# Eleven quads of edges get their rows by one SyncE transfer per edge instead of four GpSimd gathers

## The chip, the cores and the metric

The kernel runs on one core of a Trainium2 chip. A core has five instruction streams that work side by side and wait for one another by semaphores: TensorE (PE, matmul), VectorE (DVE), ScalarE (ACT), GpSimd (POOL) and SyncE (SP), and 16 DMA engines that move data for all of them. The metric is the device time of one execution in microseconds (us).

## What is computed

A graph layer with 12500 nodes and 400000 edges, sorted by destination. All is in 32-bit floats.

```python
h_s, h_v = s @ lin1_ws * a * ..., einsum('nci,cd->ndi', v, lin1_wv) * a * ...   # per node: 160 numbers
hid = silu(edge_scalars @ fc_w1 * _inv(R))                                      # per edge
w1, w2, w3, w4, w5 = split(hid @ fc_w2 * _inv(FC_HID), [64, 128, 160, 192])
es, ev = h_s[edge_src], h_v[edge_src]                                           # gather by source
m_s1 = w1 * es * e0
m_s2 = w4 * einsum('eci,ei->ec', ev, e1) * _inv(3)
m_v1 = (w2 * es)[:, :, None] * e1[:, None, :]
m_v2 = w3[:, :, None] * ev * e0[:, :, None]
m_v3 = w5[:, :, None] * cross(ev, e1[:, None, :]) * _inv(2)
agg = segment_sum(concatenate([...]), edge_dst) * inv_nn                        # scatter by destination
pre = self_connection + agg @ lin2 * a
out = layernorm(x + concatenate([silu(pre_s[:, :64]), sigmoid(pre_s[:, 64:96])[:, :, None] * pre_v]))
```

The row of a source node, 160 floats or 640 bytes, has to be fetched once per edge. This fetch is what the change is about.

## The kernel before

**Stages.** First the node table `h_tab` (12500 rows of 640 bytes, in HBM) is made, with the transposed node features loaded in blocks, some 80 us. Then comes the edge loop, which fills nearly all of the span. At its end the last nodes are normalised and written.

**The edge loop.** 400000 edges are 3125 tiles of 128. Four tiles are a *quad*, and one pass of the loop (`for n, (c, i, tiles) in enumerate(steps)`) handles a quad; there are 782. Six quads are a *chunk* of 24 tiles, for which the edge scalars come as one tile `es` of 128 partitions (two buffers, two transfers of 384 KB, L228). Indices (`idx`, L184) and edge features (`eat`, L185) come for 72 tiles at a time, also into two buffers.

For quad n the loop does this, in order:

- `fetch(n + 4)` asks for what quad n + 4 needs of `es`, `idx` and `eat`.
- `gather` (L423) has GpSimd issue four indirect DMAs (L427), each of which fetches 128 rows of `h_tab` by the indices of one tile into the buffer `hg`. `hg` has four buffers, so GpSimd can be up to four quads ahead of the products that read them.
- `weights` (L432) has TensorE make the edge weights in PSUM, `pw` (L440). `pw` has two buffers.
- `select_quad` (L498) has VectorE write a one-hot of the destinations into spare columns of `pw` (L504) and multiply it by the edge features into `sel` (L507).
- `products` (L444) has VectorE multiply `pw` by `hg` into `pr`: one wide product (L450) and three more (L458). Between them VectorE adds finished blocks into the accumulator `acc` (L546).
- `sum_up` for the quad two before has TensorE multiply `sel` by `pr` into `pa` (L514), which is the sum by destination inside a block of three tiles.
- `hide(n + 2)` has TensorE and ScalarE make the hidden layer of a later quad (L418, L420) on every second quad.
- Finished blocks are copied from `pa` (L709, ScalarE), transposed (L523, TensorE), copied again (L526, L528), multiplied by the second weights (L538) and copied (L541). Nodes whose sums are complete are normalised in groups of four tiles (`finish`, L549): loads of `x` (L562), stores of the result (L614) after L611. Now and then a piece of the self connection is added (L683, L685, L689, L690).

**What sets the order.** TensorE, VectorE, ScalarE and GpSimd run the loop in the order in which it is written (`manual_schedule`, L781). SyncE is not in that list: the order of its loads and stores there is set by the scheduler. Register loads for the places in `acc` are made on VectorE (L733: up to 16 values for one group of blocks).

Of the kernel before, what the change touches and what calls it, by code (L numbers as in the profile page):

```python
# [10 lines left out]
F32 = mybir.dt.float32  # L11
I32 = mybir.dt.int32
I16 = mybir.dt.int16
BF16 = mybir.dt.bfloat16
AF = mybir.ActivationFunctionType
OP = mybir.AluOpType
AX = mybir.AxisListType
ENG = mybir.EngineType
PSUM = bass.MemoryType.PSUM

P = 128
# [3 lines left out]
D = S + V3  # L25
# [6 lines left out]
Q = 4  # L32
# [2 lines left out]
CT = 2 * SIDE  # L35
AHEAD = 3 * CT
NF = 4

MARGIN = 128
NO = 16  # L40
# [13 lines left out]
def gnn_kernel(  # L54
# [21 lines left out]
    nc = tc.nc  # L76
    N = x.shape[0]
# [3 lines left out]
    GT = src.shape[2]  # L81
# [7 lines left out]
    h_tab = dram.tile([N, D], F32, name="h_tab")  # L89
# [7 lines left out]
        engines={ENG.PE, ENG.DVE, ENG.Activation, ENG.Pool, ENG.SP}))  # L97
# [65 lines left out]
    steps = []  # L163
# [10 lines left out]
    def ahead(t):  # L174
        a0 = t // AHEAD * AHEAD
        if a0 not in aheads:
            n = min(AHEAD, TT - a0)
            idx = loads.tile([P, AHEAD], I32, name="idx")
            eat = loads.tile([P, AHEAD, 4], F32, name="eat")
            k = 0  # L180
            while k < n:
                g, u = divmod(a0 + k, GT)
                m = min(n - k, GT - u)
                nc.sync.dma_start(idx[:, k:k + m], src[g][:, u:u + m])  # L184
                nc.sync.dma_start(eat[:, k:k + m].rearrange("p t k -> p (t k)"),  # L185
                                  ea[g].rearrange("p t k -> p (t k)")[:, 4 * u:4 * (u + m)])
                k += m
            aheads[a0] = a0, idx, eat
        return aheads[a0]

    def index(t):
        a0, idx, _ = ahead(t)
        return idx[:, t - a0:t - a0 + 1]
# [26 lines left out]
    def load_chunk(c):  # L220
        if c in ess:
            return
        t0, halves = chunks[c]
        es = ess[c] = loads.tile([2 * S, SIDE * P], F32, name="es")
        for half, n in enumerate(halves):
            to = es[half * S:(half + 1) * S]
            e0 = (t0 + half * halves[0]) * P
            nc.sync.dma_start(to[:, :n * P], es_t[:, e0:e0 + n * P])  # L228
# [34 lines left out]
    with tc.tile_pool(name="nodes", bufs=len(starts)) as nodes, tc.tile_pool(  # L263
        name="nodes_ps", bufs=6, space=PSUM
# [40 lines left out]
        for c0, cn, quarters, cq, xa, xz in loaded:  # L305
# [6 lines left out]
            for t0 in range(0, nt, U):  # L312
                ps = nps.tile([P, U, P], F32, name="hp")
                for t in range(t0, min(t0 + U, nt)):
                    n = min(P, cn - t * P)
                    nc.tensor.matmul(ps[:n, t - t0], xa[:, t * P:t * P + n], l1,
                                     start=True, stop=True)
                k = min(U, full - t0)
# [3 lines left out]
                if t0 + k < nt <= t0 + U:  # L322
                    n = cn - full * P
# [4 lines left out]
            k = quarters * V  # L328
            for u in range(-(-cq // P)):
                n = min(P, cq - u * P)  # L330
# [10 lines left out]
            if cn > full * P:  # L341
                n = cn - full * P
# [29 lines left out]
    for to, part, pieces, w, r0, c0, by in maps:  # L372
        for k, piece in enumerate(pieces):
# [3 lines left out]
            m = terms.setdefault((to, part, four), len(terms))  # L377
# [31 lines left out]
    def hidden(pool, psum, es, halves, t0, n):  # L409
# [5 lines left out]
        for k, c0, c1 in ((2 * S, 0, ends[1]), (S, ends[1], ends[0])):  # L415
            if c1 > c0:
                c = slice(c0 * P, c1 * P)
                nc.tensor.matmul(ph[:k, c], w1[:k, :k], es[:k, t0 * P + c0 * P:t0 * P + c1 * P],  # L418
                                 start=True, stop=True)
                nc.scalar.activation(hid[:k, c], ph[:k, c], AF.Silu, scale=1.0 / math.sqrt(64))  # L420
        return hid

    def gather(pool, idx):  # L423

        hg = pool.tile([P, Q, D], F32, name="hg")
        for t, i in enumerate(idx):
            nc.gpsimd.indirect_dma_start(  # L427
                out=hg[:, t, :], out_offset=None, in_=h_tab,
                in_offset=bass.IndirectOffsetOnAxis(ap=i, axis=0))
        return hg  # L430

    def weights(psum, hid, slots):  # L432

        pw = psum.tile([P, Q, 256], F32, name="pw")
        n = len(slots)
        for t in range(0, n, 2):
            half, c = slots[t]
            m = min(2, n - t)
            assert half == 0 and all(slots[t + k] == (k, c) for k in range(m))
            nc.tensor.matmul(pw[:, t:t + m, :NWT], hid[:m * S, c * P:(c + 1) * P], w2[:m * S, :m],  # L440
                             start=True, stop=True)
        return pw
# [105 lines left out]

    def finish(fin, psum, t0, nt, p, most=NF):  # L549

# [27 lines left out]
        def gates():  # L578
            z, sg = held[:2]
            nc.scalar.activation(sg[:, :nt], z[:, :nt, :V3], AF.Sigmoid)  # L580

# [21 lines left out]
        def root():  # L603
            mv, rs = held[4:]
            nc.scalar.activation(rs[:, :nt], mv[:, :nt, 1], AF.Sqrt, bias=eps)  # L605

        def norm():
# [12 lines left out]
    tiles_of_nodes = -(-N // P)  # L620
    LAST = NF
    jobs = [(t, min(NF, tiles_of_nodes - LAST - t), P)
            for t in range(0, tiles_of_nodes - LAST, NF)]
    last_job = (tiles_of_nodes - LAST, LAST, N - (tiles_of_nodes - 1) * P)

    with tc.tile_pool(
        name="fin", bufs=1
    ) as fin, tc.tile_pool(
        name="late", bufs=2
    ) as late, tc.tile_pool(name="edge", bufs=2) as edge, tc.tile_pool(  # L630
        name="deep", bufs=4
    ) as deep, tc.tile_pool(name="pw_ps", bufs=2, space=PSUM) as pw_ps, tc.tile_pool(
        name="pa_ps", bufs=2, space=PSUM
# [24 lines left out]
        def fetch(n):  # L658

            if n < len(steps):  # L660
                c, i, tiles = steps[n]
                if i == 0:
                    load_chunk(c)
                for t, _, _ in tiles:
                    ahead(t)

        def hide(n):

# [109 lines left out]
                    turning.extend(job[:nt])  # L778
                    doing.extend(job[nt:])

        with tc.manual_schedule(engines={ENG.PE, ENG.DVE, ENG.Activation, ENG.Pool}):  # L781
            fetch(0)
            hide(0)
            waits = []
            pieces = list(range(0, N, CHN))
            products_due = []
            checks = farthest(late)
            for n, (c, i, tiles) in enumerate(steps):
                if 2 <= n < 2 + ZP // 2:
                    for k in range(2):  # L790
                        clear(2 * (n - 2) + k)
                if n in checks:
                    checks[n]()
                fetch(n + 4)
                hg = gather(deep, [index(t) for t, _, _ in tiles])
                pw = weights(pw_ps, hids[c, i // 2], [(half, u - i // 2 * 4) for _, half, u in tiles])

                rest = turning.pop(0)() if turning else None
                step_on = not rest and doing.pop(0) if doing and not turning and not rest else None
                ready = []  # L800

                def first(n=n):
                    if rest:
                        rest()
                    ready.extend(add_up(n))

                sel = select_quad(edge, tiles, pw)
                pr = products(edge, pw, hg, len(tiles), [first, lambda n=n: ready.extend(add_up(n))])
                for a in ready:
                    add(*a)  # L810
                if step_on:
                    step_on()
                begin()
                waits.append((tiles, pr, sel))
                if len(waits) > 2:
                    sum_up(n, *waits.pop(0))
                hide(n + 2)
                for blocks, in due(maps_due, n):
                    output(n, blocks)
                for j, sa in due(turns_due, n):  # L820
                    turn_blocks(n, j, sa)
                if products_due:
                    products_due.pop(0)()()
                if n % 30 == 13 and pieces:
                    products_due.extend([lambda: (lambda: None)] * 3 + self_connection(pieces.pop(0)))
            assert not pieces and not products_due
            last_steps = finish(fin, misc_ps, *last_job, most=LAST)
            n = len(steps)
            while waits:
                sum_up(n, *waits.pop(0))  # L830
            while turns_due or maps_due:
                n += 1
                for blocks, in due(maps_due, n):
                    output(n, blocks)
                for j, sa in due(turns_due, n):
                    turn_blocks(n, j, sa)
            assert len(adds) <= NO
            n += 2
            while adds:
                for a in add_up(n) + add_up(n):  # L840
                    add(*a)
            while turning or doing or to_do:
                begin()
                for f in turning:
                    f()()
                for f in doing:
                    f()
                turning.clear()
                doing.clear()
            for f in last_steps[:LAST]:  # L850
                f()()
            for f in last_steps[LAST:]:
                f()
# [4 lines left out]
        with tc.For_i(0, n_redo, 1):  # L858
# [9 lines left out]
            with tc.For_i(0, n_again, 1) as g, tc.For_i(0, GT, 1) as k:  # L868
                t = g * GT + k
# [20 lines left out]
                hg = gather(deep, [idx])  # L890
# [12 lines left out]
                with tc.For_i(first, last + 1, W) as base:  # L903
# [10 lines left out]
                    nc.vector.tensor_scalar_add(r, r, -float(W))  # L914
            for pool, job, most in [(fin, job, NF) for job in jobs] + [(fin, last_job, LAST)]:
                job_steps = finish(pool, misc_ps, *job, most=most)
# [50 lines left out]
```

## Time and profile before

| | |
|---|---|
| median of three runs | 5207.48 us (5172.77 to 5221.05) |
| the profiled execution | 5221.05 us, of which the span from first to last instruction is 5219.2 us |
| mean granted TensorE clock in it | 0.872 |
| busy: TensorE, VectorE, ScalarE, GpSimd | 77%, 47%, 18%, 57% of the span |
| gathers | 3125, from 78.9 to 5176.5 us after the start |
| moved by DMA | 411.78 MB, 256.20 MB of it by the gathers' queue |

How to read the profile: it is one execution as the hardware profiler recorded it. A line of the groups has the source line, the engine, the operation, what it writes and reads, how often, then busy time in us, the mean of one in ns, and the idle time of that engine just before these instructions with what ended most of it. "issue" is idle time in which the engine waited for nothing that the profile shows; "remote" is a wait that a semaphore ended of which no instruction was found just then. Starts and ends of matmuls are partly modelled. A timeline's lines start with the start and the duration in us. The engine names with a q (SPq, DVEq) are the instructions of that engine's sequencer, such as issuing a DMA or loading registers.

### The profile page before, as it was taken

The page shows a single profiled execution, that of the slowest core. Times are in us where ns is not written, and L with a number is a line of the kernel's source. Part 1 is how long each engine was busy: PE and PEld are TensorE (multiplying, and loading weights), DVE is VectorE, ACT ScalarE, POOL GpSimd, SP SyncE. Part 2 cuts the span into 40 slices and gives each one's busy share as a digit, 9 for nine tenths or more (in the row PEclk, how much of TensorE's full clock was granted, in tenths as well). Part 3 has the DMA queues.
Part 4 walks back from the last instruction along what each step waited for, and adds up shares of the span by engine and source line. Part 5 has one row for each costly group of instructions (what it writes and reads, how often), then busy time and mean ns, then how long its engine had stood idle before and what let it go on. Part 6 is the DMA issues. An engine that isn't in the chain of part 4 may idle for free. (4 is left out here: it accounts for less than half of the span.)

```text
span 5219.2 us, 47675 instructions
## 1 busy us (share of the span) xinstructions
PE 4008.8 (77%) x14291; PEld 1714.8 (33%) x14291; DVE 2436.4 (47%) x6584; ACT 924.8 (18%) x2463; POOL 2980.2 (57%) x3134
## 2 busy tenths in 40 slices
PE   5777777787787877867777787877877787777776
PEld 3333333333333333333333333333333333333333
DVE  4444444444444444545445444444444444444544
ACT  1211111211111111211111111111111111111112
POOL 3565555555555556655556555555555555566563
PEclk7888888898888988889988888888888898889898
DMA  7333333333323323323333333333333333333322
GB/s 189 72 73 76 78 75 79 77 76 80 75 71 77 84 68 80 85 69 85 75 74 86 73 77 82 75 77 79 78 74 78 77 76 79 75 73 86 73 71 50
DMA packets 241214, 411.78 MB, mean 79 GB/s; under 512 B 74201, under 2 KB 171877, under 8 KB 240821
## 3 DMA queue, kind: packets, MB, share of 16 engines
q0 software_dynamic: 150000, 256.20, 20.2%
q1 hardware_dynamic: 77666, 142.75, 11.5%
q10 hardware_dynamic: 13282, 9.69, 0.6%
q8 instruction: 118, 1.93, 0.2%
q14 instruction: 148, 1.20, 0.1%
HBM read 392.40 MB, written 16.00 MB: 78 GB/s over the span
## 5 line engine op out<-in xcount | busy, mean ns | idle before, releaser
L427 POOL DMA_INDIRECT hg<-h_tab,idx x3125 | 2975.5, 952 | 2196.6 <-issue 952.4
L440 PE MATMUL pw<-w,hid 128*128 128x448 f32 x3126 | 1523.7, 614 | 309.3 <-issue 113.2
L514 PE MATMUL pa<-pr,sel 128*64 128x416 f32 x6250 | 1383.7, 555 | 118.8 <-issue 72.3
L504 DVE TENSOR_TENSOR pw<-rel,iota 128x64 f32<-128x64 int16 x782 | 181.1, 232 | 2494.8 <-remote 1243.8
L458 DVE TENSOR_TENSOR pr<-pw,hg 128x384 f32<-128x384 f32 x2346 | 1152.4, 545 | 0.1
L440 PEld LDWEIGHTS pw<-w,hid 128*128 128x128 f32 x3126 | 611.4, 213 | 852.7 <-issue 680.7
L514 PEld LDWEIGHTS pa<-pr,sel 128*64 128x64 f32 x6250 | 406.8, 144 | 1030.7 <-issue 959.0
L523 PE MATMUL pt<-ident,sa 128*128 128x128 f32 x2084 | 363.6, 301 | 390.9 <-ACT hid L420 218.5
L709 ACT COPY sa<-pa 128x416 f32<-128x416 f32 x521 | 265.5, 510 | 1944.0 <-remote 793.1
L450 DVE TENSOR_TENSOR pr<-pw,hg 128x512 f32<-128x512 f32 x782 | 531.0, 679 | 1.5
L418 PE MATMUL ph<-es,w 128*128 128x512 f32 (+1 forms) x784 | 451.5, 658 | 67.4 <-ACT tt L528 35.7
L523 PEld LDWEIGHTS pt<-ident,sa 128*128 128x128 f32 x2084 | 259.5, 152 | 723.3 <-issue 327.5
L538 PE MATMUL po<-tt,l 128*96 128x256 f32 (+5 forms) x1496 | 390.8, 413 | 102.5 <-ACT tt L528 63.7
L420 ACT ACTIVATE hid<-ph 128x512 f32<-128x512 f32 x392 | 234.5, 598 | 1049.7 <-remote 556.5
L507 DVE TENSOR_TENSOR sel<-pw,eas 128x256 f32<-128x256 f32 x782 | 331.5, 424 | 43.8 <-ACT eas L486 0.6
L538 PEld LDWEIGHTS po<-tt,l 128*96 128x96 f32 (+1 forms) x1496 | 249.8, 180 | 267.1 <-issue 96.0
L526 ACT COPY tt<-pt 128x192 f32<-128x192 f32 x521 | 166.0, 319 | 911.2 <-remote 295.9
L418 PEld LDWEIGHTS ph<-es,w 128*128 128x128 f32 x784 | 119.4, 192 | 334.7 <-issue 258.3
L546 DVE TENSOR_TENSOR acc<-acc,os 96x32 f32 x1042 | 194.3, 186 | 25.4 <-ACT os L541 6.9
L528 ACT COPY tt<-pt 128x64 f32<-128x64 f32 x521 | 116.7, 224 | 0.0
L689 PE MATMUL psc<-xv,scv 96*96 96x500 f32 x50 | 39.5, 884 | 82.6 <-ACT hid L420 63.3
L573 PE MATMUL pp<-ident,acc 96*128 96x96 f32 x196 | 37.1, 275 | 82.9 <-DVE acc L546 29.7
(77 smaller groups left out, 674.4 us busy)
## 6 DMA issues: line engine op xcount, KB each, us to landing
es<-in_es_t_dram SPq DMA_DIRECT2D x260, 384.0 KB
hg<-h_tab,idx POOLq DMA_INDIRECT x3125
h_tab<-ht ACTq DMA_DIRECT2D x6, 1280.0 KB
xt<-in_x_dram SPq DMA_DIRECT2D x23, 320.0 KB
out_dram<-y SPq DMA_DIRECT2D x23, 320.0 KB
xv<-in_xv_t_dram SPq DMA_DIRECT2D x25, 187.5 KB
xs<-in_xs_t_dram SPq DMA_DIRECT2D x25, 125.0 KB
xa<-in_xs_t_dram SPq DMA_DIRECT2D x12, 256.0 KB
```

What stands on the lines that cost most here:

```text
L418: nc.tensor.matmul(ph[:k, c], w1[:k, :k], es[:k, t0 * P + c0 * P:t0 * P + c1 * P], start=True, stop=True)
L420: nc.scalar.activation(hid[:k, c], ph[:k, c], AF.Silu, scale=1.0 / math.sqrt(64))
L427: nc.gpsimd.indirect_dma_start(out=hg[:, t, :], out_offset=None, in_=h_tab, in_offset=bass.IndirectOffsetOnAxis(ap=i, axis=0))
L440: nc.tensor.matmul(pw[:, t:t + m, :NWT], hid[:m * S, c * P:(c + 1) * P], w2[:m * S, :m], start=True, stop=True)
L450: nc.vector.tensor_mul(two, pw[:, :n, :2 * S].rearrange("p t (k c) -> p t k c", k=2), hg[:, :n, None, :S].to_broadcast([P, n, 2, S]))
L458: nc.vector.tensor_mul(pr[:, :n, first:first + V3].rearrange("p t (i c) -> p t i c", i=3), pw[:, :n, None, 2 * S + k * V:2 * S + (k + 1) * ...
L507: nc.vector.tensor_mul(sel[:, :n], oh[:, :, None, :].to_broadcast([P, n, 4, W]), by_slot(tiles[0][0])[:, u:u + n, :, None].to_broadcast([P ...
L514: nc.tensor.matmul(pa[half * ROWS:(half + 1) * ROWS, :NPR], sel[:, t].rearrange("p k w -> p (k w)"), pr, start=start, stop=stop)
L523: nc.tensor.transpose(pt[:, four * P:four * P + k], sa[:k, c:c + P], ident[:k, :k])
L538: nc.tensor.matmul(po[:, k, :nb], l2[r, terms[to, part, four]], a[:, :nb], start=(n == 0), stop=(n == len(of) - 1))
L546: nc.vector.tensor_add(window, window, os[:, :, b])
L709: nc.scalar.copy(sa, pas.pop(j)[:, :NPR])
```

## The change

Quads 76, 144, 212 and so on to 756 (every 68th, eleven in all) are no longer gathered by GpSimd. For each of them SyncE

- loads the 4 x 128 indices, one row of 128 per tile, 74 quads before the quad itself (for the first, at the loop's second quad);
- after VectorE has multiplied them by 640 (66 quads before), reads them 16 at a time into registers and issues one transfer of 640 bytes per index from `h_tab` into a buffer of its own, `hq` (one buffer). One such job of 16 rows follows every second quad, 32 jobs for an own quad, so that SyncE is at it in 64 of 68 quads.

`products` then reads `hq` in the place of `hg` for that quad. SyncE is added to the engines that run the loop in the written order.

```diff
+OWN = 68
+BATCH = 16
+EVERY = 2
...
+    own = [n for n in range(OWN + 8, len(steps) - 4, OWN) if len(steps[n][2]) == Q]
+    by_bytes = h_tab.rearrange("n d -> (n d)").bitcast(U8)
+    row_bytes = 4 * D
+
+    def places(pool, n):
+
+        at_bytes = pool.tile([Q, P], I32, name="at_bytes")
+        for k, (t, _, _) in enumerate(steps[n][2]):
+            g, u = divmod(t, GT)
+            with nc.allow_non_contiguous_dma(reason="the indices of one tile"):
+                nc.sync.dma_start(at_bytes[k:k + 1], src[g][:, u:u + 1].rearrange("p u -> u p"))
+        return at_bytes
+
+    def rows_of(pool, at_bytes):
+
+        hq = pool.tile([P, Q, D], F32, name="hq", bufs=1)
+        flat_hq = hq.rearrange("p t d -> p (t d)").bitcast(U8)
+
+        def job(t, p0):
+            _, values = nc.values_load_multi_w_load_instructions(
+                at_bytes[t:t + 1, p0:p0 + BATCH], engines=[ENG.SP], min_val=0,
+                max_val=(N - 1) * row_bytes,
+                skip_runtime_bounds_check_because="every entry of src is the index of a node")
+            for p, v in enumerate(values, p0):
+                nc.sync.dma_start(flat_hq[p:p + 1, t * row_bytes:(t + 1) * row_bytes],
+                                  by_bytes[ds(v, row_bytes)][None])
+
+        return hq, [lambda t=t, p0=p0: job(t, p0) for t in range(Q) for p0 in range(0, P, BATCH)]
...
+        def fetch_rows(n):
+
+            for m in own:
+                if n == max(1, m - OWN - 6):
+                    at_of[m] = places(mine, m)
+                if n == m - OWN + 2:
+                    nc.vector.tensor_scalar_mul(at_of[m], at_of[m], float(row_bytes))
+                    hq_of[m], jobs = rows_of(mine, at_of[m])
+                    rows_due.extend((m, job) for job in jobs)
+            if n % EVERY == 0 and rows_due:
+                rows_due.pop(0)[1]()
+            assert all(m > n for m, _ in rows_due)
...
-        with tc.manual_schedule(engines={ENG.PE, ENG.DVE, ENG.Activation, ENG.Pool}):
+        with tc.manual_schedule(engines={ENG.PE, ENG.DVE, ENG.Activation, ENG.Pool, ENG.SP}):
...
                 fetch(n + 4)
-                hg = gather(deep, [index(t) for t, _, _ in tiles])
+                fetch_rows(n)
+                hg = hq_of.pop(n) if n in own else gather(deep, [index(t) for t, _, _ in tiles])
```

More of the change, by code (lines that the diff above doesn't have):

```diff
@@ L14 @@
 BF16 = mybir.dt.bfloat16
+U8 = mybir.dt.uint8
 AF = mybir.ActivationFunctionType
@@ L628, in gnn_kernel @@
     ) as fin, tc.tile_pool(
+        name="mine", bufs=2
+    ) as mine, tc.tile_pool(
         name="late", bufs=2
@@ L665, in fetch @@
                     ahead(t)
+        at_of, hq_of, rows_due = {}, {}, []
+        def fetch_rows(n):
[9 more added lines that the diff above has]
+            assert all(m > n for m, _ in rows_due)
         def hide(n):
```

## The prediction

> **What bounds the kernel now.** I read the page's busy table first, then its groups, then the waits, then GpSimd's and VectorE's timelines in one stretch. The busy table names no engine that is full:
>
> ```profile
> PE 4008.8 (77%) x14291; PEld 1714.8 (33%) x14291; DVE 2436.4 (47%) x6584; ACT 924.8 (18%) x2463; POOL 2980.2 (57%) x3134
> ```
>
> The groups carry busy time, the mean of one, and the engine's idle time before it:
>
> ```profile
> L427 POOL DMA_INDIRECT hg<-h_tab,idx x3125 | 2975.5, 952 | 2196.6 <-issue 952.4
> L440 PE MATMUL pw<-w,hid 128*128 128x448 f32 x3126 | 1523.7, 614 | 309.3 <-issue 113.2
> L504 DVE TENSOR_TENSOR pw<-rel,iota 128x64 f32<-128x64 int16 x782 | 181.1, 232 | 2494.8 <-remote 1243.8
> L450 DVE TENSOR_TENSOR pr<-pw,hg 128x512 f32<-128x512 f32 x782 | 531.0, 679 | 1.5
> ```
>
> GpSimd does nothing but gathers. 2975.5 + 2196.6 = 5172.1 us lie from the first gather's neighbourhood to the last, so its timeline is the span but for 47 us. Of the idle time 952.4 us is "issue", 0.305 us before each gather, which no one can remove. A gather therefore costs 0.952 + 0.305 = 1.257 us, a quad of four 5.03 us, and the 3125 together 3928 us. The other 1244 us are waits for VectorE to give back an `hg` buffer. VectorE in turn idles 2495 us before L504, its first step of a quad, and only 1.5 us before L450, the first to read gathered rows: it never waits for rows, always for TensorE's `pw`. So each seems to wait for the other. The timelines (start us, duration us, engine and line, idle time before) show how:
>
> ```profile
> 2610.22 1.01 POOL L427 DMA_INDIRECT hg<-h_tab,idx  x1 [5.48 <-DVE acc L546]
> ...
> 2622.79 0.95 POOL L427 DMA_INDIRECT hg<-h_tab,idx  x1 [0.30 <-issue]
> 2624.04 0.95 POOL L427 DMA_INDIRECT hg<-h_tab,idx  x1 [0.30 <-issue]
> 2626.01 0.94 POOL L427 DMA_INDIRECT hg<-h_tab,idx  x1 [1.03 <-DVE acc L546]
> 2627.26 0.95 POOL L427 DMA_INDIRECT hg<-h_tab,idx  x1 [0.30 <-issue]
> 2628.51 0.95 POOL L427 DMA_INDIRECT hg<-h_tab,idx  x1 [0.30 <-issue]
> 2629.77 0.95 POOL L427 DMA_INDIRECT hg<-h_tab,idx  x1 [0.30 <-issue]
> 2635.93 0.94 POOL L427 DMA_INDIRECT hg<-h_tab,idx  x1 [5.21 <-DVE pw L504]
> ```
>
> ```profile
> 2626.82 1.67 PE L440 MATMUL pw<-w,hid 128*128 128x448 f32 x4
> ```
>
> ```profile
> 2615.00 0.23 DVE L504 TENSOR_TENSOR pw<-rel,iota 128x64 f32<-128x64 int16 x1 [0.39 <-PE pw L440]
> 2623.06 0.23 DVE L504 TENSOR_TENSOR pw<-rel,iota 128x64 f32<-128x64 int16 x1 [5.06 <-PE pa L514]
> 2632.97 0.23 DVE L504 TENSOR_TENSOR pw<-rel,iota 128x64 f32<-128x64 int16 x1 [6.91 <-remote]
> ```
>
> GpSimd issues 16 gathers almost without a pause and then stands still. TensorE's `pw` was over at 2628.5, yet L504 starts at 2632.97, 2.25 us after the last gather's end at 2630.72. I counted this over the trace. For each quad whose L504 found VectorE idle, I took the time from the modelled end of its last L440 matmul to L504, and the place of the gather under way in its unbroken run (pauses under 0.5 us). Among the first six gathers of a run, 49 of 271 quads are late by over 0.5 us and the median is 0.04; from the eighth on it is 188 of 190, median 8.7 us. Of all 296 late ones (mean 6.7 us) 120 end between 2.0 and 3.3 us after GpSimd's last gather. I don't know the mechanism, but the order of cause is plain: TensorE's results reach the others late during a long run of gathers, and come when GpSimd runs out of buffers. A turn is then GpSimd's run plus a stall, and a shorter list of gathers shortens the runs.
>
> **The change, part by part.** *Removed:* eleven quads (76, 144, ... 756) lose four gathers each; the built program lists 44 fewer on GpSimd and the same work on TensorE. 44 x 1.257 = 55.3 us of GpSimd's timeline. What becomes of the 1244 us of stalls is not shown. Bounds: they grow by all that is removed, gain 0; or they shrink with the gathers, 44 x (1.257 + 1244/3125) = 72.8. A stall comes when four gathered quads wait, and VectorE must still work through the extra quad (about 2.8 us, which its 47% leaves room for), so I take the stalls as they are: 55.
>
> *Added on VectorE:* eleven multiplications of 4x128 indices. Not in the trace; the nearest rows are 0.17 (L609) to 0.23 us (L504). 2 us, kept on the path since VectorE releases GpSimd. Each also waits for its four index loads, which are issued eight quads (52 us) ahead. Behind it stands that quad's L504, and after it GpSimd. Row loads land in `hq`, and L450 of an own quad waits for them.
>
> *Added on SyncE:* 352 jobs, one in two quads (2 x 5172/782 = 13.2 us), each a load of 16 registers and 16 row transfers; with the 44 index loads that makes 5676 more transfers beside some 640 now. The nearest rows:
>
> ```profile
> L733 DVEq TENSOR_LOAD <-rows x68: 535/1099/2299, 196.9 to 5200.0; - x68
> L185 SPq DMA_DIRECT2D eat<-in_ea_dram x68: 327/423/1495, 65.3 to 4922.1; - x68
> L228 SPq DMA_DIRECT2D es<-in_es_t_dram x262: 465/532/1087, 65.8 to 5128.2; - x131
> ```
>
> L733 reads 1042 / 68 = 15.3 values at a time (durations: shortest/median/longest, ns), so 1.10 us for 16. An issue with the gap to the next (0.05) costs 0.38 to 0.58; a row address in a register is in no row, and I take 0.45. A job is then 1.10 + 16 x 0.45 = 8.3 us, at worst 1.10 + 16 x 0.58 = 10.4. SyncE's own issues add about 0.7 us per job. It fits into 13.2 and hides behind the quads. Without that cover it would be 352 x 8.3 = 2.9 ms.
>
> A limit of another kind: each transfer waits for the one eight before it, as they share eight semaphores. From issue to the last count on its semaphore the trace has 2.05 us for `eat` (median), 4.05 for `idx`, 4.94 for `es` (95%: 6.03). A one-row transfer is nearest to `eat`: 2.05 / 8 = 0.26 per transfer, below the issue. At the end of 6.03 it would be 0.75, a job 13.1.
>
> [...] A gather here moves 80 KB, a row 640 bytes. [...]
>
> *Moved:* SyncE's order is now as written. `es` is asked for four quads before its chunk and read two quads before, 13 us, against 4.94 to land. `idx` is asked for four quads ahead, while GpSimd may gather it one quad later (6.6 us against 4.05). In the old trace an `idx` load went out at 2441 and its edge features were sorted at 2577, 136 us later. SyncE must also pass stores that wait for L611 and the first job of each own quad, which waits for VectorE. A job (8.3) behind such a wait eats most of either margin; GpSimd's lateness there replaces a stall it would have had anyway. I take 0; the price if not is below.
>
> *Sum:* 55 - 2 = 53. The profiled execution took 5221 (span 5219.2), so 5168 for its like. That execution is the slowest of the three and 13.6 above their median, so against the median: 5154.
>
> **Rivals.** *The stalls take it back.* TensorE has the largest share, and if its work sets the pace the eleven quads end no sooner: 5207. For it, 77% and a granted clock of 0.87; against it, L504's lateness follows GpSimd's run. 0.18.
>
> *SyncE falls behind.* The point is a job of 13.2 - 0.7 = 12.5 us, 0.71 per transfer, a landing of 5.7. At 6.03 a job is 13.1 and each of the 352 is 0.6 over: 211 us, everything behind SyncE (`es`, then L418 and all of TensorE) late by it: 5207 + 211 = 5418. For it, `es` lands so late; against it, 384 KB are not 640 bytes. 0.09.
>
> *Late results get later.* If the row transfers lengthen each of the 296 late releases as gathers do, 0.18 us each cancels the gain, and 0.5 us each costs 148: 5154 + 148 = 5302. For it, the cause of lateness is unknown and may be transfers in flight; against it, `es` loads of 768 KB fall in stretches where L504 is prompt (2633.1). 0.08.
>
> *The written order.* 43 `idx` loads and 130 chunks: 1 us late each puts 173 on: 5327. It decides above 0.3 us. For it, margins fall from 136 us to some 26; against it, SyncE runs ahead between waits. 0.07.
>
> That the gathers stay is excluded by the instruction list.
>
> **How the numbers follow.** The forecast gets 0.58. Its own range: stalls shrinking with the gathers, 5207 - 73 + 2 = 5136; half the gain, 5181; three runs spread over 48 us, so 15 more on either side: 5120 to 5195. One per cent of 5207 is 52 us (about what a measurement of this kernel can tell from no change), so the forecast lies on that line, and I put 0.36 of its chance beyond it, as shorter stalls pass it clearly and half the gain is the rarer way to miss. Within 1%: the other 0.22, the first rival's 0.18, and 0.04 for small forms of the other three: 0.44. Slower: the 0.20 left of their 0.24. The range takes the forecast, the first rival and the milder half of the slow cases: 5110 to 5300.
>
> **What would show it.** Right: L427 x3081 with 0.95 and 0.305 as now, its waits for VectorE still near 1240, L450 still without idle time, SyncE's issue near 0.4 us. Wrong: those waits grown by 50 (first rival); the timeline's jobs back to back over 12.5 us (second); mean lateness above 6.7 us (third); L427 waiting for `idx`, or L418 for `es` (fourth).

## The result, and the profile after

The changed kernel took 5392.86 us (median of four runs, 5380.75 to 5413.62), the kernel before 5202.31 beside it: a ratio of 1.0376 [1.0313, 1.0438]. The forecast was 5154, so both its sign and its range (5110 to 5300) missed. The profiled execution after has a span of 5380.5 us against 5219.2. In the changed kernel's numbering L427 is L431, L440 is L473, L450 is L483, L458 is L491, L504 is L537, L546 is L579; the row transfers are L460, their register loads L455.

The busy table and the groups of the kernel after:

```profile
PE 4021.5 (75%) x14291; PEld 1736.1 (32%) x14291; DVE 2438.5 (45%) x6595; ACT 920.3 (17%) x2463; POOL 2938.4 (55%) x3090
```

```profile
L431 POOL DMA_INDIRECT hg<-h_tab,idx x3081 | 2933.6, 952 | 2390.5 <-issue 939.4
L473 PE MATMUL pw<-w,hid 128*128 128x448 f32 x3126 | 1522.8, 615 | 244.8 <-ACT hid L424 138.1
L537 DVE TENSOR_TENSOR pw<-rel,iota 128x64 f32<-128x64 int16 x782 | 180.7, 231 | 2597.5 <-remote 1468.9
L483 DVE TENSOR_TENSOR pr<-pw,hg 128x512 f32<-128x512 f32 x771 | 523.6, 679 | 3.2 <-issue 1.1
```

The 44 gathers are gone and each of the rest costs what it did (952 ns). But GpSimd's waits for others are 2390.5 - 939.4 = 1451 us where they were 1244: +207. With -55 for the gathers that is +152 of the 161 by which the span grew. VectorE waits longer before L537 and still not before L483: it waits for TensorE, not for rows. The waits (us in total, times, longest) show that GpSimd still waits for VectorE's steps above all:

```profile
DVE pw L537 <- remote: 1468.9, 168, 17.5
...
POOL hg L431 <- DVE acc L579: 750.6, 155, 11.5
...
POOL hg L431 <- DVE pr L491: 381.2, 81, 8.7
...
POOL hg L431 <- DMA hq<-h_tab: 61.1, 11, 10.4
...
POOL hg L431 <- DMA idx<-in_src_dram: 8.7, 2, 4.4
```

The last two rows are new: before the change no gather waited for a load of SyncE's. No gather reads `hq`. SyncE's loads share eight semaphores (numbers 100 and 102 to 108 in the trace), and at eight of these 13 waits the gather is the first of a new block of 72 tiles and starts when the index load for it has landed (six of the eight stand under `hq`). Of the +207, then, 70 us stand behind SyncE's loads, 19 behind two waits for a multiplication of indices (L710), and the remaining 118 behind VectorE's usual steps.

One turn in the timelines of GpSimd, VectorE and TensorE after (start, duration, idle time before):

```profile
3196.03 0.94 POOL L431 DMA_INDIRECT hg<-h_tab,idx  x1 [4.82 <-DVE pw L537]
...
3202.28 0.94 POOL L431 DMA_INDIRECT hg<-h_tab,idx  x1 [0.31 <-issue]
...
3209.78 0.95 POOL L431 DMA_INDIRECT hg<-h_tab,idx  x1 [0.30 <-issue]
3216.22 1.01 POOL L431 DMA_INDIRECT hg<-h_tab,idx  x1 [5.49 <-DVE acc L579]
```

```profile
3213.27 0.23 DVE L537 TENSOR_TENSOR pw<-rel,iota 128x64 f32<-128x64 int16 x1 [10.01 <-remote]
```

```profile
3201.70 1.77 PE L473 MATMUL pw<-w,hid 128*128 128x448 f32 x4
```

TensorE's `pw` is over at 3203.5, in the sixth gather of the run (that of 3202.28); L537 starts at 3213.27, 2.5 us after the twelfth and last gather. Before the change a release in the sixth gather was late in 41% of the cases; now it is in 77%. Counted by the gather under way when `pw` ends, as in the prediction:

| gather of the run | 4th | 5th | 6th | 7th | 8th | late ones in all | mean lateness |
|---|---|---|---|---|---|---|---|
| before | .17 | .13 | .41 | .83 | .97 | 296 | 6.70 us |
| after | .23 | .49 | .77 | .92 | .96 | 295 | 6.59 us |

So late releases are neither more nor longer; they begin about one gather earlier. GpSimd also runs dry sooner: runs of 16 gathers fell from 94 to 55, pauses over 0.5 us rose from 292 to 313, and their mean from 4.31 to 4.71 us.

### The profile page after: what moved, and what is told of

Same layout as the page of the kernel before. It is cut to its first block, busy times and chain, and to the rows that moved or that the text cites. A ratio compares the mean times of both kernels' runs of the same rounds, so it can differ in the third digit from the quotient of the medians.

```text
span 5380.5 us, 59309 instructions
## 1 busy us (share of the span) xinstructions
PE 4021.5 (75%) x14291; PEld 1736.1 (32%) x14291; DVE 2438.5 (45%) x6595; ACT 920.3 (17%) x2463; POOL 2938.4 (55%) x3090
## 3 DMA queue, kind: packets, MB, share of 16 engines
q1 hardware_dynamic: 95266, 146.40, 11.7%
## 5 line engine op out<-in xcount | busy, mean ns | idle before, releaser
L431 POOL DMA_INDIRECT hg<-h_tab,idx x3081 | 2933.6, 952 | 2390.5 <-issue 939.4
L473 PE MATMUL pw<-w,hid 128*128 128x448 f32 x3126 | 1522.8, 615 | 244.8 <-ACT hid L424 138.1
L547 PE MATMUL pa<-pr,sel 128*64 128x416 f32 x6250 | 1368.0, 556 | 96.5 <-ACT sa L759 51.1
L537 DVE TENSOR_TENSOR pw<-rel,iota 128x64 f32<-128x64 int16 x782 | 180.7, 231 | 2597.5 <-remote 1468.9
L491 DVE TENSOR_TENSOR pr<-pw,hg 128x384 f32<-128x384 f32 x2313 | 1136.3, 545 | 2.4 <-issue 2.4
L473 PEld LDWEIGHTS pw<-w,hid 128*128 128x128 f32 x3126 | 616.9, 215 | 777.8 <-issue 569.1
L556 PE MATMUL pt<-ident,sa 128*128 128x128 f32 x2084 | 383.1, 313 | 583.3 <-ACT hid L424 277.9
L556 PEld LDWEIGHTS pt<-ident,sa 128*128 128x128 f32 x2084 | 271.5, 158 | 932.4 <-ACT hid L424 319.4
L422 PE MATMUL ph<-es,w 128*128 128x512 f32 (+1 forms) x784 | 464.3, 675 | 133.3 <-ACT tt L561 102.7
L483 DVE TENSOR_TENSOR pr<-pw,hg 128x512 f32<-128x512 f32 x771 | 523.6, 679 | 3.2 <-issue 1.1
L422 PEld LDWEIGHTS ph<-es,w 128*128 128x128 f32 x784 | 121.9, 196 | 400.1 <-issue 251.8
L579 DVE TENSOR_TENSOR acc<-acc,os 96x32 f32 x1042 | 194.0, 186 | 30.5 <-ACT os L574 6.7
L574 ACT COPY os<-po 96x512 f32<-96x512 f32 (+2 forms) x68 | 38.3, 563 | 419.5 <-PE po L571 124.4
```

The costliest lines, as they stand in the source:

```text
L431: nc.gpsimd.indirect_dma_start(out=hg[:, t, :], out_offset=None, in_=h_tab, in_offset=bass.IndirectOffsetOnAxis(ap=i, axis=0))
L483: nc.vector.tensor_mul(two, pw[:, :n, :2 * S].rearrange("p t (k c) -> p t k c", k=2), hg[:, :n, None, :S].to_broadcast([P, n, 2, S]))
L491: nc.vector.tensor_mul(pr[:, :n, first:first + V3].rearrange("p t (i c) -> p t i c", i=3), pw[:, :n, None, 2 * S + k * V:2 * S + (k + 1) * ...
L547: nc.tensor.matmul(pa[half * ROWS:(half + 1) * ROWS, :NPR], sel[:, t].rearrange("p k w -> p (k w)"), pr, start=start, stop=stop)
L556: nc.tensor.transpose(pt[:, four * P:four * P + k], sa[:k, c:c + P], ident[:k, :k])
L579: nc.vector.tensor_add(window, window, os[:, :, b])
```

## The experiments

Each ratio is to the kernel before in the same set of runs. The sets fell into two kinds, and no ratio below can be read without this: in some the kernel before took 5136 to 5219 us, in others 4044 to 4051 (the results name one chip number under both kinds, so it may not be the chip itself). I call them *late* and *prompt*, for the releases of TensorE; the prediction and the result above are of the late kind.

**Parts of the change, late kind.** e1_order is the kernel before with SyncE added to the written order, nothing else.

```diff
-with tc.manual_schedule(engines={ENG.PE, ENG.DVE, ENG.Activation, ENG.Pool}):
+with tc.manual_schedule(engines={ENG.PE, ENG.DVE, ENG.Activation, ENG.Pool, ENG.SP}):
```

> The kernel before, with SyncE's loop in the written order and nothing else changed. Theory A (the row transfers make TensorE's results reach the others late sooner, so that GpSimd's stalls grow by 207 us): no row transfers here, so within 20 us of before (about 5202). Theory B (the written order makes es and idx late): most of the 190 us lost, 5340 to 5400. Theory C (TensorE sets the pace and the gathers removed are worth nothing): as before, 5202.

Measured 1.0021 [0.9997, 1.0046]. By itself the written order costs nothing that stands out of the noise, 24 us at the most.

e2_fewer_gathers has the 44 gathers fewer, but no row transfers: the eleven quads read a buffer that was filled once.

```diff
-                fetch_rows(n)
-                hg = hq_of.pop(n) if n in own else gather(...)
+                hg = hq if n in own else gather(...)
```

> The changed kernel without its row transfers, index loads and multiplications: the eleven quads read a buffer that one plain load of 512 rows fills before the loop, so their products use the wrong rows; GpSimd has 3081 gathers and SyncE the written order. Theory A: the gain of the forecast without its cost, 5202 - 55 = 5147 (5130 to 5170), stalls before L431 near 1240 us. Theory B: 5290 to 5350. Theory C: 5202, the stalls grown by 55.

Measured 0.9957 [0.9924, 0.9991], some 22 us of 5219 (5 to 40), between theory A (a gain of 32 to 72 us) and C (none). The page:

```profile
L431 POOL DMA_INDIRECT hg<-h_tab,idx x3081 | 2937.2, 953 | 2210.6 <-issue 942.8
```

GpSimd's waits are 1268 us: the stalls take back part of the 55, though not all of it.

e3_rows_too keeps all gathers and lets SyncE fetch all the rows as well, for nobody.

```diff
-                hg = hq_of.pop(n) if n in own else gather(...)
+                hg = gather(...)
```

> The changed kernel with all of its row transfers, but GpSimd gathers the eleven quads as well and the products read those; hq is filled and never read. Theory A: the loss of the change without its gain, 5393 + 55 = 5448 (5420 to 5480), late releases from the fifth or sixth gather of a run instead of the seventh or eighth. Theory B: 5393 at most. Theory C: 5393, since the gathers are worth nothing.

Measured 1.0391 [1.0354, 1.0428]. The rows alone cost it all; against the change's 1.0376, of another set, the 44 gathers saved are worth some 8 us, which is within the noise, and not the 55 of theory A:

```profile
L431 POOL DMA_INDIRECT hg<-h_tab,idx x3125 | 2974.8, 952 | 2400.4 <-issue 940.7
```

e4_lighter_pe is the kernel before with half the columns in two of three L514 additions of a block, to see if TensorE's work is the pace.

```diff
+        n = NPR if start else NPR // 2
-        nc.tensor.matmul(pa[..., :NPR], ..., pr, start=start, stop=stop)
+        nc.tensor.matmul(pa[..., :n], ..., pr[:, :n], start=start, stop=stop)
```

> The kernel before with less TensorE work: the second and third tile of each block add only the first 208 of 416 columns into pa, so 208 columns of most sums lack two thirds of their edges. That takes 4166 x 0.174 us = 725 us of matmul at full clock. If TensorE's work sets the pace (C): 4500 to 4600. If GpSimd's runs and the late results set it (A): within 100 us of 5202, since the runs and the place where results turn late are as before.

Measured 1.0017 [0.9982, 1.0053], with TensorE busy for 3745 us instead of 4009: it is not.

**What of the rows costs, late kind.** All three keep every gather, the 44 index loads and the eleven multiplications, and use no row. e6_loads_only has the 352 register loads without transfers; e7_fixed_rows has 5632 one-row transfers with fixed addresses and no register loads; e8_sixteen_rows moves the same bytes in 352 transfers of 16 rows.

```diff
-            _, values = nc.values_load_multi_w_load_instructions(...)   # e7, e8
-            for p, v in enumerate(values, p0):                      # e6: loop left out
+            for p in range(p0, p0 + BATCH):                         # e7
+                v = (t * P + p) * 23 * row_bytes
                 nc.sync.dma_start(flat_hq[p:p + 1, ...], by_bytes[ds(v, row_bytes)][None])
+            r0 = (t * P + p0) * 23                                  # e8
+            nc.sync.dma_start(hq[p0:p0 + BATCH, t], h_tab[r0:r0 + BATCH, :])    # e8
```

> All gathers stay on GpSimd; SyncE loads the indices and does the 352 register loads of 16 values, but issues no row transfer. If the register loads bring the late results on sooner: 5400 to 5430, as with rows and all gathers (1.039). If it is the transfers: 5210 to 5240 (1.000 to 1.005), stalls before L431 near 1270 us.

> All gathers stay on GpSimd; SyncE issues the 5632 transfers of one row in the same bursts of 16, but from addresses fixed when the kernel is built (wrong rows, never read) and without register loads. If the transfers themselves are the cost, whatever their addresses: 5400 to 5440 (1.035 to 1.042). If addresses in registers are: 5210 to 5250.

> All gathers stay on GpSimd; each burst of 16 one-row transfers is one transfer of 16 rows from a fixed address (never read): the same bytes and the same rows of 640 bytes, 352 issues instead of 5632. If the bytes or the rows in flight are the cost: 5400 to 5440. If the count of issues and completions is: 5210 to 5250 (1.000 to 1.006).

Measured 1.0043 [1.0015, 1.0070], 1.0250 [1.0212, 1.0288] and 1.0051 [1.0018, 1.0084]. GpSimd's lines of e7 and then e8:

```profile
L431 POOL DMA_INDIRECT hg<-h_tab,idx x3125 | 2981.1, 954 | 2242.3 <-issue 948.5
```

```profile
L431 POOL DMA_INDIRECT hg<-h_tab,idx x3125 | 2973.8, 952 | 2113.6 <-issue 952.9
```

e7 lies between its two expectations; e6 and e8 came as expected if transfers are the cause. Bytes matter little; the number of transfers does. Not even the packets differ: the queue that brings the rows (q1) moved 95266 of them and 146.40 MB in e7 and in e8 alike, so the cost goes with the issues and completions. (The rows of one transfer in e8 lie side by side in `h_tab`, those of e7 do not.) What takes the step from 1.025 to 1.039 was asked of e14_loads_fixed in a later set of the late kind: register loads and transfers, with fixed addresses.

```diff
             _, values = nc.values_load_multi_w_load_instructions(...)   # kept, unused
-            for p, v in enumerate(values, p0):
+            for p in range(p0, p0 + BATCH):
+                v = (t * P + p) * 23 * row_bytes
```

> The kernel before with all gathers, the index loads, the 352 register loads and 5632 single-row transfers from fixed addresses (loaded values and rows are left unused). Where TensorE's releases come late: 1.034 to 1.040 if the register loads beside the transfers make up the difference between 1.025 (fixed addresses, no register loads) and 1.039 (true addresses with them); 1.025 to 1.030 if true addresses do. Where the releases do not come late: 0.999 to 1.001.

Measured 1.0257 [1.0202, 1.0311]: true addresses make the step, not the register loads. In the trace of the changed kernel a true address puts one more instruction on SyncE for each row, a MOVE into a register ahead of the transfer:

```profile
L460 SPq MOVE hq<-h_tab x5632: 2/29/1422, 153.3 to 5161.4; - x195
```

By the instructions that each has beyond the 47675 of the kernel before (the head of the page), the runs order themselves: e8 +387, 1.0051; e6 +405, 1.0043; e7 +5682, 1.0250; e14 +6047, 1.0257; e3 +11690, 1.0391. The first two are alike within the noise. That the addresses are also scattered was not tried apart from that.

Two things in the traces limit this account. With true addresses SyncE has less time to spare, and index loads come late: GpSimd waited for SyncE's loads for 55 us in e3, 27 in e14 and 16 in e7, so up to half of the step of some 70 us may be this. And the earlier onset of late releases goes with the cost only in part: in the sixth gather 79% are late in e3 and 68% in e14, but 40% in e7, which costs as much as e14; kernels with few transfers of rows or none have 14 to 41%. That the earlier onset is what costs the time is therefore not shown.

**Less buffering.** e5_buffers2 is the kernel before with two `hg` buffers instead of four.

```diff
-         name="deep", bufs=4
+         name="deep", bufs=2
```

> The kernel before with two hg buffers instead of four. If a turn is GpSimd's run of gathers plus a stall of some 6 us, and the late results end with the run: runs of at most 8 to 12 gathers, stalls of 4 to 6 us each, more of them; 6.2 to 8 us for a quad, so 5200 to 6200, and lateness (mean 6.7 us) falls by half. If TensorE set the pace: 5200, unchanged.

Measured, late kind, 0.9915 [0.9884, 0.9946]:

```profile
L427 POOL DMA_INDIRECT hg<-h_tab,idx x3125 | 2980.1, 954 | 2094.2 <-issue 921.9
L504 DVE TENSOR_TENSOR pw<-rel,iota 128x64 f32<-128x64 int16 x782 | 180.0, 230 | 1765.0 <-remote 825.0
```

Less buffering is worth 44 us of 5136, but not in the way expected. The runs did not get shorter (10.8 gathers in the mean, 10.7 before; 81 of them are 16 long) and the mean lateness is 6.8 us instead of half of 6.7. Late releases are fewer, 229 where the profile before has 296 and e8, of this set, 271. What brings the gain is not shown.

**The prompt kind.** The next set was meant to go on from there, with the changed kernel on two buffers (e9), half the fixed rows (e10: eight of each job's sixteen), and three buffers (e12). A fourth run, e11_loads_fixed, is the kernel of e14.

```diff
-         name="deep", bufs=4
+         name="deep", bufs=2        # e9, in the changed kernel; e12: bufs=3, in the kernel before
-            for p in range(p0, p0 + BATCH):         # e10, against e7
+            for p in range(p0, p0 + BATCH // 2):    # e10
```

> The changed kernel with two buffers for the gathered rows instead of four. Theory: the row transfers cost time by bringing the late releases on earlier within long unbroken runs of gathers, so shorter runs leave them less to spoil: in the kernel before, two buffers gave 0.9915 with 229 late one-hots instead of 296. With both, a ratio of 1.010 to 1.025 against the kernel before, and the waits of GpSimd for other engines below 1350 us (1451 in the changed kernel). Rival: the transfers hold TensorE's releases up by themselves, however long the run: then the two effects add, 1.038 less 0.0085, which is 1.027 to 1.033, and the waits stay above 1380.

> The kernel before with all gathers, and SyncE fetching rows at fixed addresses as in the run of 5632 single-row transfers (1.025), but eight in a job instead of sixteen: 2816 transfers in as many jobs. The rows are not used. If each transfer adds its own small hold-up, the cost halves: 1.012 to 1.016. If a few transfers in a run of gathers are enough to bring the late releases on, most of it stays: 1.019 to 1.025. If only a job longer than the gap between two gathers does harm (sixteen transfers took some 5 to 9 us, eight 2.6 to 4), it goes: below 1.008.

> The kernel before with all gathers, the index loads, the 352 register loads and 5632 single-row transfers; the loaded values are left unused and the transfers read fixed addresses (the rows are not used either). Fixed addresses without register loads gave 1.025, true addresses with them 1.039, register loads alone 1.0043. If the rest comes from the register loads beside the transfers, this gives 1.034 to 1.040; if from addresses that are taken from registers or scattered at random over the table, 1.025 to 1.030.

> The kernel before with three buffers for the gathered rows instead of four (two gave 0.9915). If the gain comes from GpSimd's being held sooner, so that its unbroken runs of gathers get shorter, three buffers give part of it: 0.993 to 0.999, with 240 to 285 late one-hots. If two buffers happen to be right for another reason (less held by a pause at each quad), three are no better than four, 0.998 to 1.002, with some 290 late ones.

The kernel before took 4046.34 us here, so that the premise of the four expectations, late releases, did not hold: e9 1.0613 [1.0595, 1.0631], e10 0.9992 [0.9982, 1.0001], e11 0.9992 [0.9982, 1.0001], e12 1.0010 [1.0000, 1.0019]. The page of e12, which is the kernel before but for a buffer, shows what is different:

```profile
L427 POOL DMA_INDIRECT hg<-h_tab,idx x3125 | 2979.1, 953 | 1029.3 <-issue 945.1
L450 DVE TENSOR_TENSOR pr<-pw,hg 128x512 f32<-128x512 f32 x782 | 537.5, 687 | 928.2 <-DMA hg<-h_tab,idx 927.2
L504 DVE TENSOR_TENSOR pw<-rel,iota 128x64 f32<-128x64 int16 x782 | 178.5, 228 | 500.3 <-PE pw L440 497.3
```

A gather costs what it did (953 + 302 ns), but GpSimd waits for others only 84 us, and 3125 x 1.255 = 3922 us of gathers fill a span of 4047. "remote" is gone from L504, three of 282 releases are late, and VectorE now waits for gathered rows (L450). GpSimd runs for up to 1116 gathers without a pause. So a long run of gathers does not make TensorE late by itself, and where nothing is late the rows are free (e11: 0.9992).

That the change itself is then a gain was tested by running it again. The first time fell into the late kind:

> The changed kernel once more, beside a run on whose chip the kernel before took 4046 us instead of some 5200, with GpSimd issuing its gathers almost without a pause (3125 x 1.257 us is 3928) and no late releases of TensorE. Theory: the change costs time only by way of the late releases. Where they occur, 1.033 to 1.044, as measured at first. Where they do not, the 44 gathers saved show in full and the rows cost nothing: 55 of 4046 us less, a ratio of 0.984 to 0.990. Rival: the rows or their use (the product that waits for a quad's last row, the multiply, the index loads) cost time of their own: then 1.00 or more there as well.

1.0345 [1.0291, 1.0400], as at first. The second time fell into the prompt one, with half the rows beside it:

> The changed kernel again, beside the run with half the rows. Where TensorE's releases come late: 1.031 to 1.044, as on the two chips before. Where they do not (the kernel before at some 4046 us): 0.984 to 0.990 if the change costs time by way of the late releases alone, 1.00 or more if its rows, or the wait for them, cost time of their own.

> The kernel before with all gathers and 2816 single-row transfers from fixed addresses, eight in a job instead of sixteen (the rows are not used; no register loads). Where releases come late: 1.012 to 1.016 if each transfer adds its own small hold-up, as 5632 of them gave 1.025; 1.019 to 1.025 if a few transfers in a run of gathers are enough; below 1.008 if only a job that is longer than the gap between gathers does harm. Where releases are prompt: 0.999 to 1.001, as before.

**4001.41 us against 4051.16: a ratio of 0.9879 [0.9863, 0.9896]**, and 0.9995 [0.9986, 1.0005] for e17. The page and SyncE's rows of e15_after_third, which is the changed kernel:

```profile
L431 POOL DMA_INDIRECT hg<-h_tab,idx x3081 | 2937.4, 953 | 1011.2 <-issue 926.7
L483 DVE TENSOR_TENSOR pr<-pw,hg 128x512 f32<-128x512 f32 x771 | 528.6, 686 | 799.1 <-DMA hg<-h_tab,idx 796.6
L537 DVE TENSOR_TENSOR pw<-rel,iota 128x64 f32<-128x64 int16 x782 | 179.0, 229 | 562.6 <-PE pw L473 560.7
```

```profile
L460 SPq DMA_DIRECT2D hq<-h_tab x5632: 222/228/357, 133.9 to 3814.2; - x195
```

The gain is 49.8 us of the 55.3 that 44 gathers cost, with one late release of 333. SyncE's register loads and rows in the first run of the changed kernel, the late kind:

```profile
L455 SPq TENSOR_LOAD <-at_bytes x352: 3/1220/1820, 152.0 to 5146.7; - x176
```

```profile
L460 SPq DMA_DIRECT2D hq<-h_tab x5632: 2/228/1422, 153.4 to 5161.5; - x195
```

The fields are shortest/median/longest in ns. In the prompt kind every issue takes 0.22 to 0.36 us; in the late kind they stretch. I took the time from one row's issue to the next (a register load between them included) against the gather under way:

| gather of the run | 1-2 | 3-4 | 5-6 | 7-8 | 9-12 | later |
|---|---|---|---|---|---|---|
| after, late kind: mean us per row | 0.49 | 0.78 | 1.12 | 1.40 | 1.73 | 2.15 |
| e14, one instruction fewer per row | 0.38 | 0.47 | 0.57 | 0.73 | 0.90 | 1.11 |

In the prompt kind the median is 0.32 anywhere. In the late kind the medians go to 0.7, 1.4 and 2.1 us, and in the later gathers half the instructions make half the time. It is not TensorE alone, then, that is held up during a run of gathers: SyncE is too, more with each gather.

The last set was again prompt: half the rows once more (e18), and the kernel before with two buffers (e19).

> The kernel before with all gathers and 2816 single-row transfers from fixed addresses, eight in a job (the rows are not used; no register loads). Where TensorE's releases come late: 1.012 to 1.016 if each transfer adds its own small hold-up (5632 gave 1.025); 1.019 to 1.025 if a few in a run of gathers are enough; below 1.008 if only a job longer than the gap between gathers does harm. Where releases are prompt: 0.999 to 1.001.

> The kernel before with two buffers for the gathered rows instead of four. Where releases come late it gave 0.9915, as GpSimd is held sooner and its runs of gathers get shorter: 0.988 to 0.995 again. Where they are prompt there is nothing to shorten and GpSimd only waits longer for a free buffer: the changed kernel with two buffers had 336 us of pauses there, so 1.05 to 1.08.

e18 gave 0.9998 [0.9989, 1.0007], so its question, whether half the rows cost half where releases are late, stays open. e19 gave 1.0636 [1.0621, 1.0650]:

```profile
L427 POOL DMA_INDIRECT hg<-h_tab,idx x3125 | 2989.5, 957 | 1266.9 <-issue 880.1
```

Two buffers hold GpSimd up for 387 us where three held it up for 84. The loss of e9 is that of its buffers. No version here beats both kernels in both kinds: two buffers are best in the late kind (0.9915), the change in the prompt one (0.9879).

## Why the prediction was wrong, point by point

**What bounds the kernel.** Right for the kind of run that was profiled: gathers plus stalls, and stalls by late releases. The sentence that failed is "the order of cause is plain: TensorE's results reach the others late during a long run of gathers". A run of 1660 gathers in e15 has one late release. The run is the setting; something that differs between the sets is needed too.

**"I take the stalls as they are."** This is the step that decided the miss. The stalls grew by 207 us, 70 of them behind SyncE's loads. By parts: without rows, e2 shows that they take back some 33 of the 55 (15 to 50), which is the first rival at a little over half its size; with rows, e3 shows +204 us, which nothing in the sum allowed for. Where there are no stalls (e15) the sum of 53 is nearly right: 49.8.

**SyncE.** The job was put at 8.3 us, at worst 10.4. From its register load to the end of its last issue it takes 6.8 us in the prompt kind (median). In the late kind it takes 11.2, and 20.0 at the 95% point, and 144 of the 352 are over the 12.5 us that the second rival named. SyncE kept up in the mean, as jobs start 13.3 us apart in the median, but its slack was gone. Summed over its waits for semaphores, it waited 4264 us before and 772 after. On the `es` loads, which wait for a free buffer, that was 2857 us before and 46 after (the longest row of each, L228 and L232; L455 is a job's register load):

```profile
SPq L228 <- remote: 1365.8, 51, 47.8
```

```profile
SPq L455 <- DVE pw L537: 233.5, 9, 38.4
...
SPq L232 <- PE pt L556: 31.4, 1, 31.4
```

An index load then stands behind a stretched job, and GpSimd behind the load, here for 10.4 us (the load lands at 4918.81):

```profile
4899.53 12.30 SPq L460 DMA_DIRECT2D hq<-h_tab  x13
...
4913.34 0.36 SPq L188 DMA_DIRECT2D idx<-in_src_dram  x1
```

```profile
4919.06 0.95 POOL L431 DMA_INDIRECT hg<-h_tab,idx  x1 [10.45 <-DMA hq<-h_tab]
```

Eight gathers that open a block of indices waited 48 us in this way; for `es` TensorE waited only 4.2 us (L422). So the second rival came in a small form, and "It fits into 13.2 and hides behind the quads" was wrong: an issue was put at 0.45 us and took 0.68 in the mean, since it stretches during the runs of gathers.

**Late results get later.** This was the third rival, at 0.08, and it came nearest: the row transfers do harm by way of the late releases. Its price was set at 148 us for 0.5 us on each of 296 releases; the stalls grew by 207. But the releases did not get later, so that its test, a mean lateness above 6.7 us, would have denied it: the mean is 6.59. They set in earlier, which is not shown to be all of the cost (e7). What was said against it, that large `es` loads fall where L504 is prompt, was misread at 2633.1 (the L504 of 2632.97 is 9 us late) and measured the wrong thing. A load of 384 KB is one transfer; e8 (1.0051) shows that bytes do little harm and e7 (1.0250) that issues do much.

**Written order.** "I take 0" was right for the order alone (e1), but not beside the rows: the fourth rival's sign, gathers that wait for `idx`, is there, with the 48 us above. It was argued that such a wait replaces a stall; no run separates that. **VectorE:** eleven multiplications of 0.28 us are 3 us for the 2 assumed, and GpSimd waited 19 us behind two of them.

**Many small transfers.** The prediction let 5632 one-row transfers hide in SyncE's idle time. What their number costs in the late kind is shown by e7 and e8: 1.0250 in 5632 transfers of one row, 1.0051 for the same bytes in 352 transfers of 16 rows. In the changed kernel they used up that queue's waiting (4264 us before, 772 after) and fell on others besides (70 us of GpSimd's waits stand behind SyncE's loads).

**What stays open** is what makes a set of runs late or prompt, and what the engines share in the late kind. That TensorE's work was over when the profile's model says so, and only its release came late, is also a reading: the ends of matmuls are modelled. Late releases (296 before, 295 after), SyncE's stretched instructions (0.49 us per row in the first two gathers of a run, 2.15 in the later ones) and the order by instruction count stand side by side in the late kind; no run shows what joins them. GpSimd's own pace does not differ (1.257 us and 1.255), and the number of instructions alone does not make the late kind: e15 has the same 59309 as the first run of the changed kernel, in 3992 us and with one late release. Every time here is of a recorded run (each comes with a span and a granted clock); none without the recording is at hand.

## What to carry to other kernels

An idle queue is not a free one (SyncE's waited for 4264 us before the change): count the instructions that an edit adds to any engine, and ask whom their issue and completion can hold up, and which loads stand behind them. In the late kind the same bytes cost 1.0250 row by row and 1.0051 in transfers of 16 rows. A stall whose mechanism is unknown must not enter a sum as a constant: its bound belongs on both sides. And a gain that rests on such a stall should be measured in more than one set of runs, since here the same edit is worth +3.8% or -1.2%.

## What was not expected of the hardware

- The same kernel took 5136 to 5219 us in some sets of runs and 4044 to 4051 in others, with nearly the same time per gather (1.257 and 1.255 us). The granted clock was 0.87 in the one and 0.96 in the other, with TensorE busy 77% and 91% of the span; e4 (0.826, no change in time) speaks against the clock as the cause.
- In the late kind an instruction on SyncE's queue goes from 0.3 us to steps of about 0.7 us while GpSimd gathers, and recovers in its pauses (0.32 us from row to row there, in the median).
- A one-row transfer is issued every 0.32 us with its address in a register, 0.29 with a fixed one, and a load of 16 registers takes 1.22 to 1.23 us.
